# Scans over 1024 columns and two PSUM banks in a four-layer convolution and state-space kernel

## The chip, the core and the metric

The kernel runs on one core of one Trainium2 chip, in float32 throughout. The metric is the device time of one execution in microseconds; lower is better. The times of the kernel before are the median of 3 runs, and one more execution was recorded by the hardware profiler.

## The reference

Four images of 128 channels and 128 x 128 pixels pass through four residual layers, each on group-normalised input:

```
x = x + L0(gn(x))   # deformable 3x3 convolution: 9 bilinear samples per pixel, then a matmul
x = x + L1(gn(x))   # 5x7 convolution, dilation (2,3), to 16 channels and back to 128
x = x + L2(gn(x))   # half depthwise 3x3, half a 2-D selective scan (4 directions, 16 states)
x = x + L3(gn(x))   # 3x3 convolution with a central-difference term
```

The scan of layer 2 is, for each of 4 directions, 128 channels and 16 states, a recurrence over the 16,384 pixels:

```
h = h * exp(delta * A) + (delta * u) * B      # one step per pixel
y = sum over states of h * C
```

## The kernel before, in words

An image is cut into 32 blocks of 512 pixels (`N`, `NBLK`). The state-space scan is the main thread: `scan` walks over `seq`, 4 images x 4 directions x 32 blocks = 512 blocks. A block has 128 channels x 16 states = 2,048 recurrences; they are laid out as 4 groups `j` of 4 tiles `g` (`NG`) of 128 partitions, so each block has 16 steps and each step one VectorE instruction over 512 columns, `tensor_tensor_scan` (L1071). Two of the four directions run from the last pixel to the first (`back`), with reversed access patterns.

For one group `j` the work is this:

- `states_up` (L929): TensorE spreads B into the PSUM bank `dub`. The one bank of that tag is shared in turn by `pdt`, `pxbc` and `psum` of `prepare`, which makes delta two blocks ahead.
- `inputs` (L936): VectorE multiplies delta x u by B into the tile `h`, 128 x 4 x 512. Where GpSimd is free, it does this for `j` = 3.
- `decay` (L963): ScalarE writes exp(delta x A) for one step into a PSUM bank `pa`. There are two `pa` banks, or three while `beside["spare"]` is set: the third is `bank(3)` of the side layers.
- the scan (L1071): VectorE runs over `pa` and `h`, starting from a column of `carry`.
- `carry_on` (L994) and `outputs` (L1000): the last column is kept as the next `carry`, and `h` is multiplied by C. GpSimd does both, except that VectorE does while `beside["busy"]` is "POOL", that is, beside layer 0, whose gathers GpSimd issues.
- `sums` (L974): TensorE adds the states up into `yacc`; `finish` copies it out.

The other layers are side threads. Each is a generator; `weave` cuts its work into groups, and `together` pulls groups of the side thread between the steps of the scan, in a fixed proportion. The side layers of one image run beside the scan of another: the order is layer 2's end and layer 3 of the image before, the table of layer 0, then layer 0 (gathers with L445, weights with L458 and L471), layer 1, and the start of layer 2 of the next image. Side layers have four PSUM banks of their own, `bank(0)` to `bank(3)`. All instructions of an engine run in the order in which they were recorded (`keep_order`). Waits between engines are not written by hand: the tile framework derives them from what each instruction reads and writes, tile by tile.

The central lines of the scan's inner loop before:

```
if g == 2:
    decays(at + 2)
...
o, f = h[:, g, :], c["a", n]
nc.vector.tensor_tensor_scan(o, f, o, carry[:, n : n + 1], ALU.mult, ALU.add)
```

`decays(at)` records the fills up to step `at` + 1, so a fill is recorded one step ahead of its scan.

Of the kernel before, what the change touches and what calls it, by code (L numbers as in the profile page):

```python
# [18 lines left out]
P = 128  # L19
# [93 lines left out]
def conv_preact_kernel(ctx: ExitStack, tc: tile.TileContext, a: dict, nb: int):  # L113
# [7 lines left out]
    psb = ctx.enter_context(tc.tile_pool(name="bgps", bufs=1, space=PSUM))  # L121

# [125 lines left out]
    def layer0_table(st, spare=True):  # L248
# [7 lines left out]
        with ExitStack() as s:  # L256
# [12 lines left out]
            sc, sh = yield from gn_affine(stats, 2)  # L269
# [19 lines left out]
            def turn(i):  # L289
                got["t", i] = pt = bank(2, "pt") if spare else pss.tile([P, N], F32, name="pt", tag="pa", bufs=2)  # L290
                for r in range(R):
                    nc.tensor.transpose(
                        pt[:, r * P : (r + 1) * P], got["n", i][:, r * W : (r + 1) * W], ident
                    )
# [17 lines left out]
    def layer0(st, pairs=10):  # L312
# [5 lines left out]
        with ExitStack() as s:  # L318
# [18 lines left out]
            def positions(j):  # L337
# [7 lines left out]
                po = bank(3, "po")  # L345
# [17 lines left out]
                pt = bank(3, "ptp")  # L363
# [58 lines left out]
            def lower_weights(j):  # L422

                wts = got.pop(("l", j))
                wl = bank(2, "wl")[:, 0 : 2 * ROWS * KK]
                nc.vector.tensor_mul(
                    wl.rearrange("p (q n) -> p q n", q=2),
                    wts[:, 1:2, 0].to_broadcast([P, 2, ROWS * KK]), wts[:, :, 1],
                )
                got["p"] = wl.rearrange("p (q r b k) -> p r b k q", q=2, r=R, b=BPS)  # L430
# [95 lines left out]
            fetch_strip(0)  # L526
            for n, _ in enumerate(positions(0)):
                yield share * min(1.0, (n + 1) / 21)
# [6 lines left out]
            flush()  # L535
        st["x1"], st["stats1"] = keep, stats_out


    def layer1(st):
# [3 lines left out]
        with ExitStack() as s:  # L543
# [45 lines left out]
            def rows_in(i):  # L589

                xn, top = got["n", i // BPB], strip(i)[0]
                got["p", i] = p1 = bank(i % 2 * 2, "p1")[0:M].rearrange("p (r w) -> p r w", w=W)
# [32 lines left out]
            def add(i):  # L625
# [5 lines left out]
            order = [[(0, fetch), (5, copy)], [(4, rows_in), MORE], [MORE], [(9, add)], [MORE],  # L631
                     [(2, normalise), MORE], [MORE], [(8, columns_in)], [(5, move), (6, fetch_block)]]
# [5 lines left out]
    def layer2_pre(st):  # L638
# [6 lines left out]
        with ExitStack() as s:  # L645
# [35 lines left out]
            def centre(i):  # L681
                got["d", i] = pd = bank(2, "pd2")
                nc.tensor.matmul(pd, cms, got.pop(("x", i)), start=True, stop=True)
# [8 lines left out]
            def spread_variance(i):  # L692
                got["v", i] = pv = bank(2, "pv2")
# [43 lines left out]
            def convolve(i):  # L737
# [7 lines left out]
                use = [(1, 0, 0), (0, 0, -1), (2, 0, 1), (4, 1, 0), (3, 1, -1), (5, 1, 1)]  # L745
                for n, (t, ty, tx) in enumerate(use):
                    first, final = n == 0, n == len(use) - 1
                    co, cf = span(tx, W)
                    rf = slice(1 + ty, 1 + ty + R)
                    nc.tensor.matmul(px3[:, :, co], convw[:, t, :], a[:, rf, cf], start=first, stop=final)  # L750
                    yield
                    if ty == 0:
                        nc.tensor.matmul(py3[:, :, co], diag[:, t, :], b[:, rf, cf], start=first, stop=n == 2)
                        yield

            def copy(i):
# [8 lines left out]
                yt = pp.tile([P, N], F32, name="yt")  # L765
                nc.scalar.copy(yt, got.pop(("y", i)))
                store(blk(yd, i)[low], yt[low])
                out = W if i == 0 else 0
                store(yd[HALF:P, i * N - W + out : (i + 1) * N - W], yt[HALF:P, out:])

            def gate(i):
                got["z", i] = pz = bank(2, "pz")
                nc.tensor.matmul(pz, inz, flat(got.pop(("w", i))[0][:, 1 : R + 1, :]), start=True, stop=True)

            def finish_strip(i):
# [9 lines left out]
                if "decays" in beside:  # L785
                    beside["decays"]()
# [13 lines left out]
                if (y0 + SB) % CH == 0:  # L800
                    c0 = y0 + SB - CH
                    for q in range(4):
# [5 lines left out]

            order = [[(6, convolve), (0, fetch), (2, centre)], [MORE], [MORE], [MORE], [(2, square)],
                     [MORE], [MORE], [(3, spread_variance)], [MORE], [MORE], [(3, invert)], [MORE],  # L810
                     [MORE], [(4, affine(-1))], [MORE], [(4, affine(0)), MORE], [(3, scale)], [(5, shift)],
                     [(4, affine(1)), MORE], [(6, copy)], [(6, gate)], [], [(6, finish_strip), MORE], [MORE], [MORE], [MORE], [MORE]]
# [5 lines left out]
    def scan(pull):  # L818
# [12 lines left out]
        ahead = {"turn": -1, "made": 0}  # L831

        def decays(at):

            beside["decays"] = lambda: decays(at + 1)
            while ahead["made"] < min(at + 2, len(seq) * NST):
# [16 lines left out]

        def prepare(t, early=False):
# [3 lines left out]
            if (st["b"], k) not in carries:  # L858
                carries[st["b"], k] = carry = small.tile([P, NST], F32, name="carry")
                nc.vector.memset(carry, 0.0)  # L860
            c["carry"] = carries[st["b"], k]
            c["bc"] = st["bc"][k % 2][i, k // 2]
            u = c["u"]
            yield
            pdt = pss.tile([P, N], F32, name="pdt", tag="dub")
            nc.tensor.matmul(pdt, wd[:, k, :], u, start=True, stop=True)  # L866
            yield

# [5 lines left out]
            yield  # L874
            nc.scalar.activation(e, e, AF.Exp, scale=-1.0)
            yield
            one_e = sp.tile([P, N], F32, name="one_e", bufs=1)
            nc.scalar.activation(one_e, e, AF.Identity, bias=1.0)
            yield
            if not back:  # L880
                px = pss.tile([P, N], F32, name="pxbc", tag="dub")
                nc.tensor.matmul(px, xbc[:, k, :], u, start=True, stop=True)
            ln = sp.tile([P, N], F32, name="ln", bufs=1)
            nc.scalar.activation(ln, one_e, AF.Ln)
            yield
            if not back:
                bc = sp.tile([4 * NST, N], F32, name="bc", bufs=1)
                nc.scalar.copy(bc, px[0 : 4 * NST])
                store(st["bc"][k][i].rearrange("d j s t -> (d j s) t"), bc)
            nc.scalar.activation(one_e, one_e, AF.Identity, bias=minus)  # L890
            yield
            yield
            if not early:
                yield
                yield
# [3 lines left out]
            yield  # L899
            if not early:  # L900
                yield
# [3 lines left out]
            yield  # L905
            if early:
                yield
# [44 lines left out]
        def decay(n):  # L952

            t, n = divmod(n, NST)
            j, g = divmod(n, NG)
            k = seq[t][1]
            turn = (ahead["turn"] + 1) % 3
            if turn == 2 and not beside.get("spare"):
                turn = 0
            ahead["turn"] = turn  # L960
            pa = bank(3, "pa3") if turn == 2 else pss.tile([P, N], F32, name="pa", bufs=2)
            at = g * NG + j
            nc.scalar.activation(pa, blocks[t]["d", g], AF.Exp, scale=neg_a[:, k, at : at + 1])  # L963
            blocks[t]["a", n] = pa
# [24 lines left out]
        def carry_on(t, j, engine=nc.gpsimd):  # L989
# [4 lines left out]
            copy(blocks[t]["carry"][:, j * NG : (j + 1) * NG].unsqueeze(2), h[:, :, end : end + 1])  # L994
# [22 lines left out]
        decays(-1)  # L1017
        slots = len(seq) * NST
        for t, (st, k, i, back) in enumerate(seq):
            c = blocks[t]  # L1020
            carry = c["carry"]
            on_vector = beside.get("busy") == "POOL"
            c["by"] = nc.vector if on_vector else nc.gpsimd
            more = prepare(t + 2, on_vector) if t + 2 < len(seq) else iter(())
            if t > 0:
                fetch(t + 3)
            for j in range(NG):
# [3 lines left out]
                if ("h", j) not in c:  # L1031
                    inputs(t, j, nc.vector)
                h = c["h", j]
                if t + 1 < len(seq) and j in (1, 2):
                    spread_steps(t + 1, j - 1)
                at = t * NST + j * NG
                decays(at)
                if j == 1 and t + 1 < len(seq):
                    spread_inputs(t + 1)
                if j == 2 and t + 1 < len(seq):  # L1040
                    spread_outputs(t + 1)
                if j == 3 and back:
                    c["before"] = load(sp, blk(st["y"][k % 2], i), [P, N], "before", bufs=1)
                for g in range(NG):
                    n = j * NG + g
                    if g == 1:
                        decays(at + 1)
                        if t + 1 < len(seq) and j == 3:
                            spread_steps(t + 1, 2)
                            spread_steps(t + 1, 3)  # L1050
                        if t + 1 < len(seq) and j == (2 if c["by"] is nc.gpsimd else 3):
                            spread_products(t + 1)
                        next(more, None)
# [5 lines left out]
                    if n and g in (0, 3):  # L1059
                        next(more, None)  # L1060
                    if g == 3 and then[0] < len(seq) and not (then[1] == NG - 1 and c["by"] is nc.gpsimd):
                        states_up(*then)
                    if g == 2:
                        decays(at + 2)
                        if j == 0 and c["by"] is nc.gpsimd:
                            inputs(t, NG - 1, nc.gpsimd)
                        next(more, None)
                    o, f = h[:, g, :], c["a", n]
                    if back:
                        o, f = o[:, ::-1], f[:, ::-1]  # L1070
                    nc.vector.tensor_tensor_scan(o, f, o, carry[:, n : n + 1], ALU.mult, ALU.add)  # L1071
                    if g == 3:
                        decays(at + 3)
                        if j == 1 and t > 0:
                            finish(t - 1)
                    yield (t * NST + n + 1) / slots
# [11 lines left out]
    def layer2_post(st, engine=nc.gpsimd):  # L1088
# [6 lines left out]
        with ExitStack() as s:  # L1095
# [44 lines left out]

            def centre(i):
# [10 lines left out]
            def square(i):  # L1152
                p = got["p", i]
                got["d", i] = d = pp.tile([P, N], F32, name="d3", bufs=3)
                if engine is nc.gpsimd:
                    nc.scalar.copy(d, p)
                    got["p", i] = d
# [7 lines left out]
            def invert(i):  # L1165
                rsqrt(got["s", i], got.pop(("v", i)), out_eps)
# [12 lines left out]
            def project(i):  # L1179

                got["q", i] = pj = bank(2, "pj3")
# [3 lines left out]
            def square_out(i):  # L1185
                p = got["q", i]
                got["e", i] = d = pp.tile([P, N], F32, name="d4", bufs=4)
                if engine is nc.gpsimd:
                    nc.scalar.copy(d, p)
                    got["q", i] = d  # L1190
# [311 lines left out]
```

## Time and profile before

| | |
|---|---|
| time, median of 3 runs | 21086.46 us (21069.96 to 21094.95) |
| the profiled execution: its own time | 21033.39 us |
| its span, first to last instruction | 21031.6 us |
| granted TensorE clock, mean | 0.881 |
| VectorE busy | 16808.6 us (80%) |
| TensorE matmul busy | 16025.3 us (76%) |
| GpSimd busy | 15945.9 us (76%) |
| ScalarE busy | 13477.7 us (64%) |
| the 8,192 scans, VectorE L1071 | 9967.9 us, 1266 ns each |
| the 8,192 fills, ScalarE L963 | 5551.9 us, 686 ns each |

From the times at which the lines of each layer are busy the span falls into these stretches: 0 to 2280 us, layers 0 and 1 of the first image, with no scan beside them; 2280 to 3480, 5440 to 8750, 10545 to 13790 and 15470 to 20650, the scan beside layers 1, 2 and 3 and the table; 3480 to 5440, 8750 to 10545 and 13790 to 15470, the scan beside layer 0; 20650 to the end, layer 3 of the last image alone.

How to read the lines: a group of instructions has its source line, engine, operation, output and inputs, shapes and count, then its busy time and the mean of one, then the time for which the engine sat idle just before them and what ended most of that. A timeline line has start, length, engine, line and operation, and in brackets the idle time ahead of it and what ended it.

### The profile page before, as it was taken

What the parts mean: (1) busy time and instruction counts of PE and PEld (TensorE: products, weight loads), DVE (VectorE), ACT (ScalarE), POOL (GpSimd) and SP (SyncE); (2) the same over time, 40 slices, a digit from 0 to 9 for tenths busy, and PEclk for the clock granted to TensorE, in tenths of its full rate; (3) what the DMA queues carried; (4) which work ended last, traced back from release to release, by engine and by line L of the source; (5) the groups of instructions that cost most, each with busy time, mean ns of one, the idle gap of its engine ahead of it and who ended that gap; (6) DMA issues with size and microseconds to landing.
All of it is one profiled execution on the core that took longest, in us unless ns stands there. A gap on an engine that the chain in (4) does not pass through costs nothing.

```text
span 21031.6 us, 207094 instructions
## 1 busy us (share of the span) xinstructions
PE 16025.3 (76%) x58778; PEld 6877.1 (33%) x58778; DVE 16808.6 (80%) x14665; ACT 13477.7 (64%) x26854; POOL 15945.9 (76%) x9469
## 2 busy tenths in 40 slices
PE   4667776777877788777787887877777877777778
PEld 2444222444322223344432222344432222222223
DVE  1222588888998899888899889978889888999983
ACT  3444676676667776566667775666666766655563
POOL 3664477666788888767768888867768889999994
PEclk7788887988988889889898998989988988789899
DMA  7666568777756777777776696777776677555673
GB/s 234 192 193 184 162 202 282 249 256 250 245 192 204 213 236 246 246 249 249 254 237 196 202 251 217 262 241 252 256 242 204 205 208 216 185 185 191 196 220 123
DMA packets 2869274, 4641.27 MB, mean 221 GB/s; under 512 B 1088976, under 2 KB 1361944, under 8 KB 2791200
## 3 DMA queue, kind: packets, MB, share of 16 engines
q1 hardware_dynamic: 2499488, 3419.78, 50.9%
q0 software_dynamic: 368640, 1208.25, 18.2%
q8 instruction: 470, 7.70, 0.1%
q14 instruction: 676, 5.54, 0.1%
HBM read 3682.39 MB, written 874.52 MB: 217 GB/s over the span
## 4 chain that ended last, share of the span: by engine, by line
PE 24%; DVE 22%; ACT 14%; issue 13%; POOL 11%; DMA 8%; another core or an unknown queue 6%; SPq 2%; DVEq 0%; POOLq 0%; ACTq 0%
DVE h L1071 12%; DVE h L936 8%; POOL h L1000 7%; PE pst L481 6%; ACT g L458 5%; PE dub L929 3%; PE psum L898 3%; ACT pa L963 3%; PE yacc L974 2%; DMA du<-stepsd 2%; DMA delta<-stepsd 2%; PE p L1297 2%; POOL h L936 2%; PE acc L496 2%
## 5 line engine op out<-in xcount | busy, mean ns | idle before, releaser
L1071 DVE TENSOR_TENSOR_SCAN h<-pa,carry,h 128x512 f32<-128x512 f32 x8192 | 9967.9, 1266 | 474.7 <-ACT pa L963 236.8
L963 ACT ACTIVATE pa<-delta,neg_a 128x512 f32<-128x512 f32 x8192 | 5551.9, 686 | 3911.7 <-DVE h L1071 3239.1
L1000 POOL TENSOR_TENSOR h<-h,cb 128x2048 f32<-128x2048 f32 x1692 | 7666.8, 4531 | 136.5 <-POOL carry L994 0.6
L445 POOL DMA_INDIRECT g<-table,idx x4608 | 4814.8, 1045 | 2317.7 <-issue 1477.3
L936 DVE TENSOR_TENSOR h<-du,dub 128x2048 f32<-128x2048 f32 x1625 | 3697.9, 2276 | 1455.8 <-PE dub L929 1000.3
L481 PE MATMUL pst<-ident,g 128*128 128x128 f32 x18432 | 2705.1, 309 | 1641.8 <-ACT smp L490 1015.5
L481 PEld LDWEIGHTS pst<-ident,g 128*128 128x128 f32 x18432 | 2449.0, 161 | 2537.7 <-ACT smp L490 1405.8
L929 PE MATMUL dub<-u,xb_sb 128*128 128x512 f32 x3250 | 2046.4, 715 | 1478.8 <-ACT above L873 960.5
L974 PE MATMUL yacc<-h,gather_sb 128*32 128x512 f32 x16384 | 2468.7, 677 | 868.9 <-POOL h L1000 609.6
L458 ACT ACTIVATE g<-g,wt 128x128 f32<-128x128 f32 x9216 | 2869.2, 392 | 58.6 <-DMA g<-table,idx 47.7
L490 ACT COPY smp<-pst 128x512 f32<-128x512 f32 x1152 | 668.3, 580 | 2104.0 <-remote 1637.9
L936 POOL TENSOR_TENSOR h<-du,bb 128x2048 f32<-128x2048 f32 x423 | 1925.2, 4551 | 16.8 <-DMA du<-stepsd 15.8
L471 DVE TENSOR_TENSOR g<-g,wl 128x512 f32<-128x512 f32 x2304 | 1484.1, 669 | 171.1 <-DMA g<-table,idx 151.2
L994 POOL COPY carry<-h 128x4 f32<-128x4 f32 x1692 | 332.0, 196 | 1535.8 <-DVE h L1071 1479.3
L929 PEld LDWEIGHTS dub<-u,xb_sb 128*128 128x128 f32 x3250 | 580.8, 212 | 2522.8 <-ACT above L873 1377.2
L496 PE MATMUL acc<-smp,w_sb 128*128 128x512 f32 x2304 | 1318.9, 656 | 49.4 <-DVE x L503 36.2
L1297 PE MATMUL p<-xn,w_l_sb 128*128 128x508 f32 (+2 forms) x2304 | 1198.4, 638 | 1.8 <-ACT xn L1276 1.8
L503 DVE TENSOR_TENSOR x<-acc,xres 128x512 f32<-128x512 f32 x128 | 87.7, 685 | 1351.7 <-remote 478.9
L974 PEld LDWEIGHTS yacc<-h,gather_sb 128*32 128x32 f32 x16384 | 343.9, 113 | 2445.9 <-POOL h L1000 1075.9
L908 POOL TENSOR_TENSOR steps<-steps,u 128x512 f32<-128x512 f32 x512 | 658.7, 1286 | 326.1 <-ACT steps L904 313.6
L866 PE MATMUL pdt<-u,wd 128*128 128x512 f32 x1024 | 635.6, 706 | 278.0 <-DVE h L936 266.2
L750 PE MATMUL px<-win,convw_sb 128*128 128x508 f32 (+1 forms) x1536 | 806.8, 623 | 26.9 <-DMA win<-win 24.0
(171 smaller groups left out, 17914.0 us busy)
## 6 DMA issues: line engine op xcount, KB each, us to landing
cb<-bcd SPq DMA_DIRECT2D x512, 1024.0 KB
delta<-stepsd SPq DMA_DIRECT2D x2048, 256.0 KB
du<-stepsd SPq DMA_DIRECT2D x2048, 256.0 KB
stepsd<-steps SPq DMA_DIRECT2D x512, 512.0 KB
table<-gt SPq DMA_DIRECT2D x512, 256.0 KB
bb<-bcd SPq DMA_DIRECT2D x512, 256.0 KB
g<-table,idx POOLq DMA_INDIRECT x4608
u<-urow SPq DMA_DIRECT2D x256, 256.0 KB
```

Source lines behind the costliest of these rows:

```text
L445: nc.gpsimd.indirect_dma_start(out=g[:, r].rearrange("p q c -> p (q c)"), out_offset=None, in_=table, in_offset=bass.IndirectOffsetOnAxis( ...
L458: nc.scalar.activation(g[:, r, c, :], g[:, r, c, :], AF.Copy, scale=wv[:, 2 * h + r, q, k, c : c + 1])
L471: nc.vector.tensor_mul(g, g, wl.unsqueeze(3).to_broadcast([P, 2, 2, P]))
L481: nc.tensor.matmul(pst[:, r * P : (r + 1) * P], g[:, r % 2, q, :], ident, start=q == 0, stop=q == 3, is_transpose=True,)
L496: nc.tensor.matmul(got["a", i], w0[:, k, :], got.pop(("c", n)), start=k == 0, stop=k == KK - 1)
L929: nc.tensor.matmul(p, xb[:, seq[t][1], j, :], c["u"], start=True, stop=True)
L936: engine.tensor_mul(h, c["du"], b.unsqueeze(1).to_broadcast([P, NG, N]))
L963: nc.scalar.activation(pa, blocks[t]["d", g], AF.Exp, scale=neg_a[:, k, at : at + 1])
L974: nc.tensor.matmul(c["y"][g * Q : (g + 1) * Q, :], gather, c["h", j][:, g, :], start=j == 0, stop=last and not second,)
L1000: engine.tensor_mul(h, h, c["cb"][:, j, :].unsqueeze(1).to_broadcast([P, NG, N]))
L1071: nc.vector.tensor_tensor_scan(o, f, o, carry[:, n : n + 1], ALU.mult, ALU.add)
L1297: nc.tensor.matmul(dst, wt, src, start=n == 0, stop=n == len(jobs) - 1)
```

## The change

One PSUM tile `four` of four banks takes the place of the `pa` banks. Steps are joined in pairs: a scan runs over 1024 columns, two tiles `g` of `h` and two neighbouring banks of `four`. So that the second half of a pair does not continue from the first, the factor at the seam is zero (written once per pair of banks and direction; the fill leaves that column out), and the second half's own carry is added by ScalarE ahead of the scan: `join` does head = head + carry x exp(delta x A) on one column, with the factor from `first`. Pairs alternate between banks 0-1 and 2-3. While layer 0 runs (`beside["narrow"]`), banks 2 and 3 are its own (`wl`, `po`, `pt`) and the scan falls back to 512 columns on banks 0 and 1. The side layers keep two banks, `bank(0)` and `bank(1)`, and their step orders are changed to suit. `states_up` and `inputs` are recorded half a group earlier, at `g` = 0 and `g` = 2 of the group before; the steps of `prepare` and the loads of delta and delta x u move accordingly.

```diff
+    four = pss.tile([P, 4, N], F32, name="four")
...
-                po = bank(3, "po")
+                po = four[:, 3]
...
-                wl = bank(2, "wl")[:, 0 : 2 * ROWS * KK]
+                wl = four[:, 2, 0 : 2 * ROWS * KK]
...
         def decay(n):
...
-            pa = bank(3, "pa3") if turn == 2 else pss.tile([P, N], F32, name="pa", bufs=2)
-            at = g * NG + j
-            nc.scalar.activation(pa, blocks[t]["d", g], AF.Exp, scale=neg_a[:, k, at : at + 1])
+            if g % 2 == 0:
+                wide = c["wide", m // 2] = not beside.get("narrow")
+                ahead["turn"] = 1 - ahead["turn"] if wide else 0
...
+            wide, pair = c["wide", m // 2], ahead["turn"]
+            c["a", m] = pa = four[:, 2 * pair + g % 2]
+            if g % 2 == 0:
+                c["aa", m // 2] = four[:, 2 * pair : 2 * pair + 2], pair
+            at = g * NG + j
+            part = slice(0, N)
+            if wide and g % 2 != back:
+                part = slice(0, N - 1) if back else slice(1, N)
...
+            nc.scalar.activation(pa[:, part], c["d", g][:, part], AF.Exp, scale=neg_a[:, k, at : at + 1])
+
+        def join(t, q):
...
+            head, n = c["h", j][:, g, edge], j * NG + g
+            nc.scalar.activation(
+                head, carry_of(t)[:, n : n + 1], AF.Identity, bias=head, scale=c["first", g][:, j : j + 1]
+            )
...
                 for g in range(NG):
                     n = j * NG + g
+                    if g == 0:
+                        if up:
+                            states_up(*then)
...
                     if g == 2:
...
+                        if up:
+                            inputs(*then, nc.vector)
...
+                    if c["wide", n // 2]:
+                        if g % 2 == 0:
+                            f, of = c["aa", n // 2]
+                            if of == 1 or not beside.get("narrow"):
+                                decays(at + g + 3)
+                            o, f = (v.rearrange("p g t -> p (g t)") for v in (h[:, g : g + 2, :], f))
+                            first = n + 1 if back else n
...
+                            nc.vector.tensor_tensor_scan(o, f, o, carry[:, first : first + 1], ALU.mult, ALU.add)
...
+                    else:
+                        decays(at + g + 1)
+                        o, f = h[:, g, :], c["a", n]
...
+                        nc.vector.tensor_tensor_scan(o, f, o, carry[:, n : n + 1], ALU.mult, ALU.add)
+                    if g == 1:
                         decays(at + 2)
+                        join(t, 2 * j + 1)
                     if g == 3:
-                        decays(at + 3)
+                        decays(at + 4)
+                        if then[0] < len(seq):
+                            join(then[0], 2 * then[1])
...
-            order = [[(0, fetch), (5, copy)], [(4, rows_in), MORE], [MORE], [(9, add)], [MORE],
-                     [(2, normalise), MORE], [MORE], [(8, columns_in)], [(5, move), (6, fetch_block)]]
+            order = [[(0, fetch), (4, rows_in), MORE], [MORE], [(9, add), MORE], [MORE], [(2, normalise), MORE], [],
+                     [(4, copy)], [(8, columns_in)], [(5, move), (6, fetch_block)]]
...
-                got["p", i] = p = bank(i % 2, "p3").rearrange("p (r w) -> p r w", w=W)
+                got["p", i] = p = bank(i % banks, "p3").rearrange("p (r w) -> p r w", w=W)
...
+            if banks == 1:
+                order = [[(0, fetch), (4, convolve), MORE], [MORE], [MORE], [MORE], [MORE], [MORE],
+                         [(2, normalise), MORE], [MORE], [MORE], [MORE, MORE, MORE, MORE], [(4, add)], [], []]
```

In the same way the orders of both halves of layer 2 change, and where VectorE serves layer 2's end, ScalarE now copies the two projections out of PSUM first (64 blocks, two copies each).

## Prediction

> **What bounds the kernel now.** I read first where the engines are busy, stage by stage. Columns: stretch in us, its length, then TensorE matmul, weight loads, VectorE, ScalarE and GpSimd busy (with counts), granted clock, DMA share, GB/s.
>
> ```profile
> 3480.00:5440.00 1960.00, 1488.18 (x7539) 862.94 (x7540) 1693.91 (x1713) 1336.23 (x3432) 1303.34 (x1191) 0.88 0.74 247
> 5440.00:8750.00 3310.00, 2672.51 (x8001) 899.86 (x8000) 3024.11 (x2363) 2238.29 (x3617) 2807.99 (x1194) 0.90 0.71 225
> 15470.00:20650.00 5180.00, 3981.49 (x11660) 1275.11 (x11660) 4769.27 (x3600) 3394.56 (x5547) 4620.89 (x2024) 0.88 0.64 203
> ```
>
> Beside layers 1 to 3 VectorE is busy 91 to 92% of the time, ahead of GpSimd (85 to 89%): what is put on VectorE's chain there is paid nearly in full. Beside layer 0 (first line) VectorE has 86%. The four stretches beside layers 1 to 3 add up to 12,935 us with 11,710 us of VectorE busy (993 + 3,024 + 2,924 + 4,769), so 1,225 us idle; the three beside layer 0 to 5,435 us with 4,506 busy and 929 idle. Next the costliest groups:
>
> ```profile
> L1071 DVE TENSOR_TENSOR_SCAN h<-pa,carry,h 128x512 f32<-128x512 f32 x8192 | 9967.9, 1266 | 474.7 <-ACT pa L963 236.8
> L963 ACT ACTIVATE pa<-delta,neg_a 128x512 f32<-128x512 f32 x8192 | 5551.9, 686 | 3911.7 <-DVE h L1071 3239.1
> L936 DVE TENSOR_TENSOR h<-du,dub 128x2048 f32<-128x2048 f32 x1625 | 3697.9, 2276 | 1455.8 <-PE dub L929 1000.3
> L471 DVE TENSOR_TENSOR g<-g,wl 128x512 f32<-128x512 f32 x2304 | 1484.1, 669 | 171.1 <-DMA g<-table,idx 151.2
> ```
>
> Scans wait for fills for only 237 us in all, though each needs one of 0.69 us: ScalarE stands ready and waits for VectorE (3,239 us), not the other way. The timeline shows how, in a dense stretch of 5 scans:
>
> ```profile
> 19004.07 5.98 DVE L1071 TENSOR_TENSOR_SCAN h<-pa,carry,h 128x512 f32<-128x512 f32 x5
> ...
> 19005.38 0.69 ACT L963 ACTIVATE pa<-delta,neg_a 128x512 f32<-128x512 f32 x1 [2.80 <-DVE h L1071]
> ...
> 19006.56 0.69 ACT L963 ACTIVATE pa<-delta,neg_a 128x512 f32<-128x512 f32 x1 [0.48 <-DVE h L1071]
> ```
>
> Scans follow each other every 1.20 us. When one ends, the fill of the bank it freed starts, and runs **under the next scan**, which has its own filled bank. And here is what an unhidden fill costs:
>
> ```profile
> 6497.50 0.63 ACT L214 ACTIVATE sq<-sq 128x512 f32<-128x512 f32 x1
> ...
> 6498.04 1.28 ACT L963 ACTIVATE pa<-delta,neg_a 128x512 f32<-128x512 f32 x2
> ...
> 6498.75 1.28 DVE L1071 TENSOR_TENSOR_SCAN h<-pa,carry,h 128x512 f32<-128x512 f32 x1 [2.03 <-ACT pa L963]
> ```
>
> The scan starts 0.71 us after its fill started.
>
> **What it removes.** 8,192 scans become 3,385 of 1024 columns and 1,422 of 512 (counted in the built program). A wide scan is in no row; it lies between 1.20 us (second half free) and 2.40 (two pitches). From 512 and 2048 columns of plain VectorE work, 0.669 and 2.276 us, the fixed part is (4 x 0.669 - 2.276)/3 = 0.133 us; I take one such part saved: 2.27 us each, 3,385 x 0.133 = 450 us less.
>
> **What it adds: a wait.** In the built program the waits of the wide scans are not what the two pairs of banks suggest. Before, every scan waits for its own fill. Now the four banks are one tile, and the waits treat it as one: a scan waits for the *last fill recorded before it*, and `decays(at + g + 3)`, on the line ahead of the scan, records the two fills of the *other* pair. Those two overwrite what the scan before has just read, and so wait for its end. The chain is: scan ends, two fills (the second also waits for the first), next scan. The overlap shown above is gone; filling and scanning take turns.
>
> How many of these are on the path is counted from the order of VectorE's instructions. Of the wide scans, 1,772 follow directly on the scan that their fills wait for: nothing covers the fills. For 1,239 the `inputs` product stands between, 2.276 us, which covers them. For 278 another product of a side layer does in part (by their rows 118 us stay open); the rest wait for nothing new. Price of an open one: 0.03 us from a scan's end (19004.07 + 1.28) to its fill's start, two fills of 0.71, and 0.06 because two scans no longer overlap (1.26 alone against 1.20 in a row): 1.5 us. From below, fills in a row as above, 1.28 + 0.05 = 1.33. 1,772 x 1.5 = 2,658 us. What stands behind the waiting scan on VectorE: `inputs` of the next group and the side layers' sums; who waits: GpSimd's `carry` and `outputs`, and through them TensorE's `sums`.
>
> Here a rule bears on it. The Trainium skill (PSUM — Partial Sum Buffer, Specifications (TRN2)) says ScalarE and VectorE can use PSUM in parallel at full bandwidth as long as they do not meet in one bank. The rows above agree for the kernel before; by the rule alone the two pairs would cost nothing here and the sum would end 2,658 us lower. The rule tells what the memory allows; the waits in the program decide. [...]
>
> **VectorE's idle time beside layers 1 to 3**, 1,225 us. Part ends: waits for fills are now in the count, and `states_up` stands half a group earlier, with slower scans besides, so that waits for `dub` (1,000 us in the whole span) shrink. Bounds: none ends, or all. I take 660.
>
> **ScalarE falls behind.** It gains 3,385 joins and 851 `first` (nearest rows: 128x1 at 0.203 and 0.251 us), some 850 us, and 128 copies of 0.58. They lie under scans. But with no fill in hand any work that ScalarE still has when a scan ends delays the next one; the table loads and Silu of layer 2 (1.28 + 1.06 + 1.04 + 1.28 us in one piece) are the worst. Bounds 0 and 850; I take 350.
>
> Sum for these stretches: -450 + 2,658 + 118 - 660 + 350 = +2,016 us.
>
> **Beside layer 0.** Scans of 512, recorded after the next step's fill, take turns with it as well; and because `wl` and `po` lie in the same tile, nearly all of those fills now wait for VectorE's last weight product L471 (1,345 in the program), and some of these products for TensorE's offset matmuls (138). 572 scans are open at 0.71 + 0.03 + 0.06 = 0.8: 458 us. The gathers on GpSimd pace this stage and VectorE idles 929 us there, so it may all be hidden; or the waits for TensorE come on top. Bounds 0 and 900; I take 300.
>
> **At nothing:** the side layers' two banks (96 `add` of layer 3 now follow the last matmuls closely; up to two matmuls, 2.06 us, each, 198 us if VectorE's new gaps did not cover them); the moved loads on SP (`du` waits were 16 us on GpSimd's product); GpSimd's 24.8 us per block (4 x 4.53, 4.55, 1.29, 4 x 0.20), covered as long as VectorE's block is longer, and it goes from about 30.4 (12,935 us for 6,805 scans, 16 to a block) to 35.
>
> **Sum.** 21,033 + 2,016 + 300 = 23,349 us for the profiled execution; the median before is 53 us above it, so 23,400.
>
> **Rivals.**
> 1. *All idle time absorbs.* Stalls at 1.33, all 1,225 us of idle gone, nothing beside layer 0: -450 + 2,357 + 118 - 1,225 = +800, some 21,900 to 22,350 in all. For it: VectorE is the only late engine then. Against: `du`, `dub` and side work still bunch. 0.12.
> 2. *ScalarE and layer 0 late too.* Both upper bounds and no idle gained: -450 + 2,658 + 118 + 850 + 900 = +4,076, at most 25,160. For it: ScalarE is in order and has 64% already. 0.12 above 24,500.
> 3. *Faster: the fills hide after all.* Place: between two wide scans. If other work covers the open waits, only the savings stay: -450 and half the idle, -612: near 20,020, or 20,400 with what ScalarE adds. It decides below a stall of (450 + 1,225)/1,772 = 0.95 us; two fills in a row take 1.28 at the least. 0.04.
>
> The likeliest case, 0.72, is 22,350 to 24,500; the range takes 100 us of each neighbour, 22,250 to 24,600. Measurement tells 0.2% from no change (the three runs lie within 25 us, 0.12%). Faster 0.03, same 0.01, slower 0.96.
>
> **What would show it.** Right: wide scans of about 2.27 us; VectorE idle before scans, ended by the fill, grown from 237 us to well over 2,000; in the timeline scan, two fills, scan without overlap; `inputs` directly between a group's two scans and no gap after it; waits for `dub` down. Wrong: fills running under wide scans, or a wide scan of 1.9 us or less, or stretches beside layer 0 longer by over 900 us.

## The result, and the profile after

The changed kernel takes 24518.77 us (median of 4 runs, 24505.05 to 24522.28); the kernel before took 21090.71 us beside it (4 runs). The ratio is 1.1625, 95% interval 1.1605 to 1.1645: 16% slower. The profiled execution took 24522.12 us, span 24520.3.

First the engines by stretch, in the changed kernel (columns as in the prediction): one stretch beside layer 0 and two beside layers 1 to 3.

```profile
3700.00:6055.00 2355.00, 1582.46 (x7472) 880.01 (x7464) 1695.01 (x1709) 1353.47 (x3429) 1259.24 (x1187) 0.83 0.62 204
6055.00:10025.00 3970.00, 2903.99 (x8001) 927.86 (x7997) 2924.08 (x1486) 2670.49 (x4778) 2820.04 (x1197) 0.85 0.60 188
...
17970.00:24140.00 6170.00, 4318.96 (x11522) 1287.17 (x11522) 4575.44 (x2156) 4023.45 (x7262) 4643.30 (x2020) 0.82 0.54 170
```

Beside layers 1 to 3 VectorE (third pair of numbers) is busy 74% of the time, where it was 91 to 92%; it does nearly the same work in a longer stretch. No engine took over as the bound: GpSimd has 71 and 75%, down from 85 and 89%. Next the costliest groups of the changed kernel:

```profile
L1117 DVE TENSOR_TENSOR_SCAN h<-four,carry,h 128x1024 f32<-128x1024 f32 x3385 | 7945.1, 2347 | 4008.7 <-ACT four L984 3933.9
L984 ACT ACTIVATE four<-delta,neg_a 128x512 f32<-128x512 f32 (+1 forms) x8192 | 5653.4, 690 | 5129.4 <-DVE h L1117 3029.5
...
L943 DVE TENSOR_TENSOR h<-du,dub 128x2048 f32<-128x2048 f32 x1625 | 3682.8, 2266 | 495.9 <-DMA du<-stepsd 289.0
...
L1125 DVE TENSOR_TENSOR_SCAN h<-four,carry,h 128x512 f32<-128x512 f32 x1422 | 1818.4, 1279 | 1222.6 <-ACT four L984 835.2
...
L472 DVE TENSOR_TENSOR g<-g,four 128x512 f32<-128x512 f32 x2304 | 1489.7, 669 | 781.2 <-issue 390.4
...
L1002 ACT ACTIVATE h<-carry,h,first 128x1 f32<-128x1 f32 x3385 | 1285.7, 380 | 661.1 <-DVE h L943 594.9
```

The first two lines wait for each other: the scans 3,934 us for fills, the fills 3,030 us for scans. Before, the fills waited too (3,239 us), which cost next to nothing, since a fill ran under the next scan; the scans waited for fills only 237 us. The granted clock of TensorE fell as well, from 0.881 to 0.836 on average, and is lower in the slower kernels here (0.865 and 0.871 in the first two of the experiments below); but VectorE waits for ScalarE's fills, and those take 690 ns on average, 686 before. The timeline of the changed kernel shows the turns:

```profile
22502.84 1.41 ACT L984 ACTIVATE four<-delta,neg_a 128x511 f32<-128x511 f32 x2 [0.78 <-DVE h L1117]
...
22504.29 2.35 DVE L1117 TENSOR_TENSOR_SCAN h<-four,carry,h 128x1024 f32<-128x1024 f32 x1 [1.48 <-ACT four L984]
...
22506.67 1.41 ACT L984 ACTIVATE four<-delta,neg_a 128x511 f32<-128x511 f32 x2 [2.11 <-DVE h L1117]
...
22508.12 2.35 DVE L1117 TENSOR_TENSOR_SCAN h<-four,carry,h 128x1024 f32<-128x1024 f32 x1 [1.48 <-ACT four L984]
...
22514.28 2.26 DVE L943 TENSOR_TENSOR h<-du,dub 128x2048 f32<-128x2048 f32 x1
...
22514.40 1.41 ACT L984 ACTIVATE four<-delta,neg_a 128x511 f32<-128x511 f32 x2 [2.18 <-DVE h L1117]
...
22516.46 2.34 DVE L1117 TENSOR_TENSOR_SCAN h<-four,carry,h 128x1024 f32<-128x1024 f32 x1
```

Scan, two fills, scan, with nothing overlapped and 1.48 us of VectorE idle each time. At the end `inputs` (L943) stands between two scans; the two fills run under it, and the scan starts without a gap.

To compare stretches between kernels, the rest of this document measures "beside layer 0" from the wait ahead of the first copy of the offset sum `po` to the last product with the lower weights, in the second to fourth image; both kernels do the same work between these rows (some 1,400 scans of 512 columns in each). "Beside layers 1 to 3" is all else between the first and the last scan. Before: 5,577 and 12,791 us; after: 6,521 and 15,316, so +944 and +2,525.

### The profile page after: what moved, and what is told of

The parts are those of the page before. It is cut to its first block, busy times and chain, and to the rows that moved or that the text cites. A ratio compares the mean times of both kernels' runs of the same rounds, so it can differ in the third digit from the quotient of the medians.

```text
span 24520.3 us, 208463 instructions
## 1 busy us (share of the span) xinstructions
PE 17195.7 (70%) x58778; PEld 7046.6 (29%) x58778; DVE 16422.1 (67%) x11280; ACT 15152.3 (62%) x31234; POOL 15921.9 (65%) x9469
## 5 line engine op out<-in xcount | busy, mean ns | idle before, releaser
L1117 DVE TENSOR_TENSOR_SCAN h<-four,carry,h 128x1024 f32<-128x1024 f32 x3385 | 7945.1, 2347 | 4008.7 <-ACT four L984 3933.9
L984 ACT ACTIVATE four<-delta,neg_a 128x512 f32<-128x512 f32 (+1 forms) x8192 | 5653.4, 690 | 5129.4 <-DVE h L1117 3029.5
L943 DVE TENSOR_TENSOR h<-du,dub 128x2048 f32<-128x2048 f32 x1625 | 3682.8, 2266 | 495.9 <-DMA du<-stepsd 289.0
L936 PE MATMUL dub<-u,xb_sb 128*128 128x512 f32 x3250 | 2328.4, 806 | 1893.6 <-DVE h L943 1129.3
L1125 DVE TENSOR_TENSOR_SCAN h<-four,carry,h 128x512 f32<-128x512 f32 x1422 | 1818.4, 1279 | 1222.6 <-ACT four L984 835.2
L1014 PE MATMUL yacc<-h,gather_sb 128*32 128x512 f32 x16384 | 2555.0, 700 | 17.9 <-POOL h L1040 11.5
L472 DVE TENSOR_TENSOR g<-g,four 128x512 f32<-128x512 f32 x2304 | 1489.7, 669 | 781.2 <-issue 390.4
L943 POOL TENSOR_TENSOR h<-du,bb 128x2048 f32<-128x2048 f32 x423 | 1913.7, 4524 | 19.8 <-DMA du<-stepsd 19.8
L885 PE MATMUL pdt<-u,wd 128*128 128x512 f32 x1024 | 842.1, 916 | 1479.4 <-DVE h L943 1432.2
L1002 ACT ACTIVATE h<-carry,h,first 128x1 f32<-128x1 f32 x3385 | 1285.7, 380 | 661.1 <-DVE h L943 594.9
L497 PE MATMUL acc<-smp,w_sb 128*128 128x512 f32 x2304 | 1385.6, 687 | 38.2 <-DVE x L504 32.0
L906 PE MATMUL psum<-e,ident 128*128 128x512 f32 x1024 | 678.3, 750 | 645.9 <-DVE h L943 631.5
```

The costliest lines, as they stand in the source:

```text
L472: nc.vector.tensor_mul(g, g, wl.unsqueeze(3).to_broadcast([P, 2, 2, P]))
L936: nc.tensor.matmul(p, xb[:, seq[t][1], j, :], c["u"], start=True, stop=True)
L943: engine.tensor_mul(h, c["du"], b.unsqueeze(1).to_broadcast([P, NG, N]))
L984: nc.scalar.activation(pa[:, part], c["d", g][:, part], AF.Exp, scale=neg_a[:, k, at : at + 1])
L1014: nc.tensor.matmul(c["y"][g * Q : (g + 1) * Q, :], gather, c["h", j][:, g, :], start=j == 0, stop=last and not second,)
L1117: nc.vector.tensor_tensor_scan(o, f, o, carry[:, first : first + 1], ALU.mult, ALU.add)
```

## The experiments

The runs fall into four groups, each on a chip of its own: the kernel before took 21,094, 21,021, 20,269 and 20,260 us in them. So each run is compared with the kernel before of its own group, by ratio, and profiles only between groups of like speed.

**One tile into two.** The instructions and their order stay; layer 0's `po`, `pt` and `wl` move into the banks of the second tile:

```diff
-    four = pss.tile([P, 4, N], F32, name="four")
+    duo = [pss.tile([P, 2, N], F32, name=f"duo{n}") for n in range(2)]
...
-            c["a", m] = pa = four[:, 2 * pair + g % 2]
+            c["a", m] = pa = duo[pair][:, g % 2]
```

> The changed kernel with the four banks given as two tiles of two banks, one for each pair; layer 0's sampling sum, its transpose and its lower weights share the second tile, the narrow fills the first. Instructions, their order, the joins, the side layers' two banks and the moved inputs are those of the changed kernel. Theory (the one tile makes each wide scan wait for fills that waited for the scan before it): the 3,934 us that the wide scans waited for fills go nearly all, under 500 us are left; of that some 500 us turn into other waits, the stretches beside layers 1 to 3 fall from 15,215 to between 11,900 and 12,900 us; beside layer 0 narrow fills still share a tile with each other but no longer with the weights and PE's sums, 6,605 falls to 5,700 to 6,400; in all 20,900 to 22,300 us, 21,500 likeliest. Rival (the wide scans, the joins of 0.38 us on ScalarE and the two banks of the side layers cost it, whatever the tiles): over 23,500 us, with the scans' waits moved to the joins.

22,206.64 us, ratio 1.0521 (1.0503 to 1.0539): 11 of the 16 points (percent of the kernel before) are gone. The total is inside the expected 20,900 to 22,300, near its upper end. Beside layers 1 to 3 the stretch is 13,248 us, 2,068 less, yet above the expected 11,900 to 12,900; beside layer 0 it is 6,305. The groups:

```profile
L1117 DVE TENSOR_TENSOR_SCAN h<-duo,carry,h 128x1024 f32<-128x1024 f32 x3385 | 7825.9, 2338 | 1074.0 <-ACT h L1002 1067.8
...
L1125 DVE TENSOR_TENSOR_SCAN h<-duo,carry,h 128x512 f32<-128x512 f32 x1422 | 1817.3, 1278 | 972.5 <-ACT duo L984 694.9
```

The waits of wide scans for fills (3,934 us) have gone; 1,068 us for joins stand in their place. The rival had the waits move to the joins; not a third of their time did, and the total is far under its 23,500 us.

**Separate tiles everywhere.** As above in the wide stretches; while layer 0 runs, the pool of the two tiles is closed and one with four tiles of one bank is open (where one follows the other, some fills are recorded one or two steps later):

```diff
+            if wide:
+                duo = banks("wide")["duo"][pair]
+                c["a", m] = pa = duo[:, g % 2]
...
+                c["a", m] = pa = single(g % 2)
...
-                po = four[:, 3]
+                po = single(3)
...
-                wl = four[:, 2, 0 : 2 * ROWS * KK]
+                wl = single(2)[:, 0 : 2 * ROWS * KK]
```

> The changed kernel with two tiles of two banks in the wide stretches and, while layer 0 runs, the same four banks as four tiles of one bank each (two for the narrow fills, one for the sampling sum, one for the lower weights), as in the kernel before. Theory: the wide stretches as with two tiles, 11,900 to 12,900 us; beside layer 0 back to the 5,435 us of the kernel before, within 250; in all 20,100 to 21,200 us, 20,600 likeliest, so somewhat faster than the kernel before. Rival for layer 0 (its 1,170 us come from the moved inputs, state matmuls and loads, not from the shared tile): those stretches stay over 6,200 us, and the whole at 21,000 to 21,900.

21,786.86 us, 1.0327 (1.0309 to 1.0344). The theory's range is missed, and a loss stands where a small gain was expected: 13,211 us beside layers 1 to 3, not 11,900 to 12,900, and beside layer 0 5,897, which is 320 more than before and yet not the rival's 6,200. In its timeline fills lie under scans again, and three wide scans follow each other with (6.83 - 2.34)/2 = 2.24 us from one to the next:

```profile
20027.69 6.83 DVE L1141 TENSOR_TENSOR_SCAN h<-duo,carry,h 128x1024 f32<-128x1024 f32 x3
...
20027.81 0.39 ACT L1027 ACTIVATE h<-carry,h,first 128x1 f32<-128x1 f32 x1
...
20030.06 1.42 ACT L1009 ACTIVATE duo<-delta,neg_a 128x511 f32<-128x511 f32 x2
```

**One tile in the wide stretches, four tiles beside layer 0.**

> The changed kernel with its one tile of four banks kept in the wide stretches, and four tiles of one bank each while layer 0 runs. Theory: the wide stretches keep their 15,215 us; beside layer 0 the 1,170 us go, 6,605 to about 5,450: 23,350 us, 23,100 to 23,700. Rival for layer 0 (moved inputs and loads): no change, 24,300 to 24,600.

23,858.34 us, 1.131 (1.1291 to 1.1329): 15,273 and 5,906 us, a little above the 23,100 to 23,700 expected, since beside layer 0 not all of the loss went. The shared tile costs 15,273 - 13,211 = 2,062 us beside layers 1 to 3, measured with separate tiles beside layer 0, and 6,521 - 5,906 = 615 us beside layer 0, measured with the one tile in the wide stretches. What each half costs depends little on the other: beside layers 1 to 3 two tiles also took 2,068 us off while layer 0 still shared them, and beside layer 0 four tiles come to 5,897 and 5,906 us. Some 420 us and 320 us of the loss have another cause (13,211 against 12,791 and 5,897 against 5,577).

**The same fault put into the kernel before**: its fills in two banks, no third, the two as halves of one tile; and, as its partner, the two banks as two tiles.

```diff
+    both = pss.tile([P, 2, N], F32, name="both")
...
-            if turn == 2 and not beside.get("spare"):
+            if turn == 2:
...
-            pa = bank(3, "pa3") if turn == 2 else pss.tile([P, N], F32, name="pa", bufs=2)
+            pa = bank(3, "pa3") if turn == 2 else both[:, turn]
```

The second kernel has only the change of the `if`. In the first, the transposes `pt` that share the banks of the fills use `both` too.

> The kernel before with the fills in two banks that are halves of one tile, and no third bank; scans of 512 columns, side layers and order as before. Theory (the shared tile alone is enough, whatever the width): every scan waits for the newest fill, and that for the scan before; a fill of 0.69 us and its handover make 0.75 us for each scan with nothing between; if about half of the 8,192 scans are open, as in the changed kernel, 3,000 to 3,400 us, of which idle time that was there may take up to half: 22,600 to 24,600 us, 23,700 likeliest. Rival (a scan and a fill run beside each other in spite of one tile): within 400 us of the kernel before.

> The kernel before without its third bank for fills: two banks in two tiles, all else as it was. It is the partner of the kernel with two banks in one tile (24,476 us). Theory: a third bank is worth little, 21,050 to 21,500 us, so that the shared tile alone costs some 3,000 to 3,400 us. Rival (the third bank carries it): over 22,500 us.

One tile: 24,476.17 us, 1.1604 (1.1584 to 1.1623), inside the theory's range. Two tiles: 21,711.12 us, 1.0328 (1.0311 to 1.0346). The shared tile alone costs 12.8 points, some 2,690 us, without a wide scan in the program, so the fault does not need the width. The rows of the scans, one tile and then two:

```profile
L1072 DVE TENSOR_TENSOR_SCAN h<-both,carry,h 128x512 f32<-128x512 f32 x8192 | 10329.8, 1277 | 4071.2 <-ACT both L964 3701.5
```

```profile
L1071 DVE TENSOR_TENSOR_SCAN h<-pa,carry,h 128x512 f32<-128x512 f32 x8192 | 10008.9, 1267 | 666.6 <-ACT pa L963 403.9
```

The third bank is worth 3.3 points, more than the expectation had.

**What is left: the joins.** Separate tiles everywhere, with the joins and their factors left out; then with the joins recorded earlier.

> The version with separate tiles everywhere (21,787 us) with the joins and their first factors left out, so the second group of each wide scan starts from its own inputs alone: that part of the recurrence is not computed. It prices the joins, for which the scans waited 1,071 us in 720 waits there. Theory (a scan waits for its join itself, 0.38 us behind late ScalarE work): nearly all of it goes, and some turns into waits for fills: 20,700 to 21,250 us, 20,950 likeliest. Rival (ScalarE's queue is late anyway, the join is only the last thing in it): the scans wait as long for the fills, 21,550 us or more.

> The version with separate tiles everywhere, with both joins of a group of inputs recorded behind the inputs, after the group's last scan before, so that the second pair's join is one wide scan earlier on ScalarE. If a late join holds the scan, about half of the 1,071 us of waits for joins go: 21,150 to 21,550 us. If ScalarE's queue is late whatever stands in it: 21,650 to 21,900.

Without joins 21,501.23 us, 1.023 (1.0213 to 1.0247). The expectations were in times of the first group; there this ratio makes some 21,580 us, at the rival's bound of 21,550. So the joins cost about one point, about 205 us, and not the 1,071 us that scans waited for them. The waits before scans fell from 1,078 to 446 us, but idle time before `inputs` rose from 1,433 to 1,836. Earlier joins gave 21,747.19 us, 1.0345 (1.0328 to 1.0363), no gain, as the second of the two expectations had it: the scans then waited 927 us for joins and 135 for fills. So a wait that ends with a join is mostly not the join's own cost. That the rest is work ahead of it in ScalarE's queue fits both runs, but was not measured piece by piece.

**What is left: the moved inputs.** Earlier joins as above, and `inputs` of the next block's first group after a block's last scan while GpSimd is busy:

> The same with earlier joins, and while GpSimd is busy with layer 0 the inputs of the next block's first group come after the last scan of a block and not before its third, as in the kernel before, since the transfer of their du is issued only two scans earlier. If the moved inputs cost the 320 us that layer 0's stretches are still longer than before with separate tiles (du waits of about 130 us in each of the three): 150 to 350 us less than with earlier joins alone. If not: within 60 us of it.

21,653.45 us, 1.0302 (1.0285 to 1.0319), 0.43 points or 90 us better, under the 150 to 350 expected. Beside layer 0 the stretch fell from 5,831 to 5,748 us; waits for `du` fell from 694 to 426 us in the whole span.

**What is left: wide scans, side layers or the order of the scan loop?** Two kernels keep the whole change without wide scans and joins (four banks, four tiles, 512 columns); two keep only its side layers, the second of them with a fourth bank for fills.

> The changed kernel without wide scans and without joins: scans of 512 columns as before, each fill in one of four banks, each bank a tile of its own, fills three scans ahead; two of the four while layer 0 runs. Side layers on two banks, the moved inputs and the new orders stay. It tells whether what is left with separate tiles (+3.3% over the kernel before) belongs to the wide scans with their joins or to the rest of the change. A third bank was worth 690 us in the kernel before. If the wide scans and joins are to blame for the rest: 20,700 to 21,150 us, at or under the kernel before. If the side layers' two banks and the moved inputs and loads are: 21,500 us or more.

> The same, and while GpSimd is busy with layer 0 the next block's first inputs come after a block's last scan, as in the kernel before. It took 90 us off the wide version; 50 to 150 us less than the four banks alone are expected if the moved inputs cost layer 0's stretches anything here, 0 if fills further ahead cover that. If wide scans and joins are to blame for what was left, this one beats the kernel before by 0.3 to 2%.

> The kernel before with the change's side layers alone: they are held to two banks and have the change's new orders and extra copies; the scans of 512 columns, their three banks, their inputs, state matmuls, loads and steps stand as before. Four banks with the whole rest of the change came to +4.2%. If the side layers' two banks cost that, this one is 3 to 4.5% slower than the kernel before. If the moved inputs, state matmuls, loads and steps cost it: within 1% of the kernel before.

> The same with the bank that is free now: the fills go round four banks beside layers 1 to 3, one more ahead, each bank a tile of its own. The third bank was worth 690 us to the kernel before; if its scans still wait for fills (475 us of idle time before them), a fourth brings 0.5 to 1.5% over three banks, and if the side layers cost nothing this version beats the kernel before. If nothing waits for fills any more: within 0.3% of three banks.

| kernel | ratio to before | interval |
|---|---|---|
| four banks, all the rest of the change | 1.0424 | 1.0410 to 1.0438 |
| the same, late inputs | 1.0301 | 1.0287 to 1.0315 |
| before, with the change's side layers | 1.0036 | 1.0023 to 1.0050 |
| the same, four banks | 1.0057 | 1.0043 to 1.0071 |

In microseconds the first two took 21,130 and 20,888, but on a chip where the kernel before takes 20,269: by the ratio, the second of the two expectations holds for the first, and the second does not beat the kernel before; it gained 242 us where 50 to 150 were expected. The side layers on two banks, with their orders and copies, cost 0.4%. The new order of the scan loop (`states_up`, `inputs`, `prepare`, the loads, and fills recorded three steps ahead) costs 3.9 points more, without a single wide scan; late inputs take 1.2 of them back. So the wide scans and joins need not be to blame for what was left: with separate tiles and wide scans it was 1.0327, a point better than with four banks, if ratios carry over from one chip to another. The two groups of these four kernels ran at the same speed, so the groups of instructions can be compared: the kernel with the side layers alone, then the four banks with all the rest.

```profile
L1073 DVE TENSOR_TENSOR_SCAN h<-pa,carry,h 128x512 f32<-128x512 f32 x8192 | 9978.3, 1266 | 450.7 <-ACT pa L965 264.7
...
L938 DVE TENSOR_TENSOR h<-du,dub 128x2048 f32<-128x2048 f32 x1625 | 3698.1, 2276 | 865.6 <-PE dub L931 750.5
```

```profile
L1126 DVE TENSOR_TENSOR_SCAN h<-one,carry,h 128x512 f32<-128x512 f32 x8192 | 9950.3, 1264 | 182.3 <-ACT one L985 179.2
...
L946 DVE TENSOR_TENSOR h<-du,dub 128x2048 f32<-128x2048 f32 x1625 | 3696.9, 2275 | 1921.6 <-DMA du<-stepsd 1047.5
```

Fills further ahead take 268 us off the scans, but idle time before `inputs` grows by 1,056 us, nearly all of it waits for the transfer of `du` (60 us in the first kernel). The net of the two, 788 us, is nearly the difference of the spans, 21,148.3 - 20,343.3 = 805. The waits of SP's queue suggest what holds `du` back. Columns: what waited and for what, us in all, times, longest; side layers alone, then four banks:

```profile
SPq L918 <- ACT pa L965: 983.8, 579, 15.4
```

```profile
SPq L926 <- ACT one L985: 3759.6, 784, 36.4
```

These are the loads of delta. The change issues the last two of a block a group earlier; they wait on SP until the last fills of the current block have read the buffers, four times as long in all as with the old order, and beside layer 0 the loads of `du` stand behind them (698 of the 1,048 us fall there). At the head of the queue the loads of `du` themselves wait less than before, 301 us for `inputs` to have read their buffer, against 1,800. The four kernels show that the order of the loop costs this much where there are no wide scans; that these two loads are what matters in it is read from the queue and was not tried alone.

A fourth bank (last row of the table) moved waits and gained nothing: before scans 451 to 259 us, for `dub` 751 to 976.

No kernel here beat the kernel before. Wide pairs in separate tiles with the old order of inputs and loads were not run, so that this order also explains the 3.3% that were left with wide scans is argued, not shown.

## Why the prediction was right, and where it was off

The direction and the mechanism held. The range held narrowly: 24,519 us is 81 us inside its upper end, 24,600. It is 1,119 us above the predicted 23,400, and 19 us above the likeliest case, in the part of the range that was given to the second rival.

Separate tiles divide the sum in two. The shared tile costs 24,519 - 21,787 = 2,732 us; the terms that belong to it (2,658 + 118 - 660 + 350 + 300, if all the idle time is counted here) make 2,766. All the rest of the change was to bring 450 us and cost 693 (21,787 against 21,094). So nearly the whole miss lies in this rest, of which the prediction had put all but the shorter scans at nothing; that the time still fell into the range, 81 us from its end, was partly luck. The same shows in the third rival: for hidden fills it had 20,020 to 20,400 us, and with the fills hidden it was 21,787. Inside the shared tile's part, too, errors cancel. Step by step, with the prediction's own cuts of the span:

- **The wait for the other pair's fills**: right, and shown, by splitting the tile, by separating it in one kind of stretch at a time and by putting the fault into the kernel before. An open wait took 1.48 us (predicted 1.5). With the 118 us and ScalarE's lateness the prediction had 3,126 us of waits before wide scans; the stretches have 3,926. The mis-sized term is ScalarE's lateness. In the trace 1,774 wide scans follow directly on a scan (1,772 were counted) and waited 3,452 us: 1,193 of them 1.51 us on average, as priced, but 580 of them 2.84 us, and in these ScalarE worked 865 us on other things ahead of the fills. So about 790 us of lateness stand against the 350 taken. The largest piece is the first two activations of delta (`e` and `above`, 314 us); the table loads and Silu, which the prediction called the worst, have some 100, and the joins 37, though joins and `first` took ScalarE 1,527 us in all (380 and 283 ns each) and not 850.
- **VectorE's idle time**: 660 of 1,225 us were to go. Besides the waits for fills only 4,074 - 3,926 = 148 us were left, so some 1,080 went, and took back half of the first error. The waits of `inputs` for `dub`, 1,000 us before, are down to 3.
- **Shorter work on VectorE**: 450 us predicted; its busy time fell by 387 (16,808.6 to 16,422.1). The rows of the scans have only 204 of that (9,967.9 against 7,945.1 + 1,818.4), since scans that wait no longer overlap; with two tiles they have 325. A wide scan alone takes 2.347 us, and 2.24 from one to the next in a row, against 2.27.
- **Beside layer 0**: +300, with bounds 0 to 900, is the step that failed. By the prediction's cuts these stretches grew by 1,170 us (6,605 against 5,435), beyond its upper bound, which is also what the prediction named as a sign that it would be wrong; 190 us of that is VectorE's work which those cuts shift between stretches, and between equal rows it is 944. The gathers did not hide the turns: between the equal rows VectorE's idle time before narrow scans grew from 144 to 1,195 us. Nearly as many scans as counted, 557 for 572, waited directly behind a weight product, 293 of them 0.82 us on average (0.8 was the price), but 264 of them 2.72; there ScalarE was late as well, 278 us of it with weight products of its own, and the prediction had no term for that. (The waits before the weight products, 781 us in the row above, are not part of this: 622 of them fall in the first image, with no scan beside them; beside scans they grew from 33 to 159.) 615 us belong to the shared tile and the other 329 do not.
- **"At nothing"**: the two banks of the side layers were nearly that, 0.4% (0.36). The moved loads and `inputs` are the other step that failed, as far as is known: VectorE waited 289 us for `du` in the changed kernel (54 before), and 592 to 639 once the stalls were gone, which seem to have covered the rest. I had looked only at GpSimd's product that waits for `du`, not at VectorE's behind the same transfer, and not at the loads of delta that hold SP's queue.
- **The rivals**: that the fills hide after all is refuted by the timeline. "All idle absorbs" had the idle time nearly right, its stall of 1.33 us and layer 0 wrong. "ScalarE and layer 0 late too" came true in these two points (layer 0's bound of 900 was passed, ScalarE's lateness came near its bound of 850) and not in the third, since the idle time went; 24,519 us is in its part of the range.

The rule that ScalarE and VectorE may use PSUM side by side as long as they do not meet in one bank (the Trainium skill, PSUM — Partial Sum Buffer, Specifications (TRN2)) agrees with these traces. With two tiles, where fills run under wide scans, a wide scan takes 2,338 ns on average, and 2,347 ns in the changed kernel, where they take turns. The banks were the same in both: the waits kept the engines apart, not the memory.

## What to carry to other kernels

Give each buffer that two engines hand to and fro a tile of its own: here the waits were derived tile by tile, and two or four PSUM banks in one tile took away the overlap between filling and scanning, at 12.8 to 13 points of time; two tiles instead of one, a change of a few lines, gave back 11. When a change moves loads earlier, look at what each waits for and at what stands behind it in the same queue (read here from the queue's waits, not tried alone); and look once more after the worst stall is gone, since a stall covers smaller ones. A wait that names the last small instruction (the join) need not be that instruction's cost: leave it out and see where the wait goes.

## What the runs showed of the hardware

- A ScalarE activation on one column, 128x1 with a per-partition scale and bias from columns, took 0.380 us (3,385 of them); the 128x1 activations of the kernel before had 0.203 and 0.251.
- The kernel before took 21,094 us on one chip and 20,260 on another, 4% apart. On the faster chips the first image's layer 0, which no scan stands beside, takes 1,438 us from its first product with the lower weights to its last; in the profile of before 1,718.
- A third bank for 0.69 us fills ahead of 1.27 us scans was worth 690 us (3.3 points), though fills are shorter than scans; a fourth, in the kernel with the change's side layers, was worth nothing (1.0057 against 1.0036).
